# Expert tiles by pairs of 128-slot units with single units for odd rests, in a woven convolution and mixture-of-experts kernel

## The chip, the cores and the metric

The kernel runs on one core of one Trainium2 chip. TensorE (PE) multiplies matrices and transposes, VectorE (DVE) and ScalarE (ACT) work elementwise, GpSimd (POOL) issues indirect DMAs (gathers by a list of row numbers), SyncE (SP) issues plain ones. The metric is the device time of one execution in microseconds; lower is better. The time before is the median of three runs.

## What is computed

```python
x = x + conv(ln_c(x))            # three deformable 3x3 convolutions, each with relu; x is (4, 256, 64, 64)
t = to_tokens(x)                 # 4 images of 4096 tokens of 256 values
t = t + ffn(ln_t(t))
x = from_tokens(t)

def ffn(xf):                     # 8 experts, the best 2 of each token
    probs = softmax(xf @ gate_w + gate_b)
    top2_vals, top2_idx = top_k(probs, 2)
    cw = zeros((N, 8)); cw[token, top2_idx] += top2_vals
    out = 0
    for w1, b1, w2, b2, we in experts:      # 256 -> 512 -> 256
        out += we[:, None] * (gelu(xf @ w1 + b1) @ w2 + b2)
    return out
```

A deformable convolution samples the image at nine computed positions a pixel, bilinearly, before its matrix product. All data is float32.

## The kernel before

The convolutions run in twelve stages (`run`, one layer of one image each), each of eight blocks of 512 pixels with nine taps a block, 864 taps in all. A tap gathers four tiles of 128 pixels by indirect DMA on POOL (`g`, line 503, ten buffers), blends them on DVE (lines 509, 514) and ACT (517), transposes them on TensorE (`tp`, 532; copied out on ACT, 535) and multiplies them into `acc` (555).

The experts are woven into this. Tokens form five groups: images 0, 1, 2 whole (32 token blocks of 128, `M` = 32), image 3 in two halves (`M` = 16). When a group's last block has its tokens, `enqueue` puts its routing on a lane, then `begin` puts its expert tiles on the lane `tiles` and `end` its combination on the lane `sums`. At each tap `pump` gives each lane a credit of one tap; a piece runs once its cost is covered. A tile has three pieces of `pace`/3 taps, with paces 5, 5, 2, 1.5 and 0 for the five groups. After the last stage the lanes are emptied tile by tile (`drain`), which is the tail; there group 3 ends and group 4 runs.

`route` counts, on DVE with two matmuls, how many (token, choice) pairs each expert has, gives each pair a slot so that each expert starts on a multiple of `FT` = 256 slots, and derives for each tile of 256 slots its expert and the rows of its weights. A group has `NF = 2*M*128/256 + 7` tiles, 39 or 23, enough for every distribution over eight experts. `invert` makes from the slots, with one-hot matrices and matmuls into `inv`, the token of each slot.

A tile f is done by `expert` and the helpers:

- `fetch` (lines 800 and 812): one indirect DMA for the weights `w` of the tile's expert (two buffers, in turn by the step's parity), and `FU` = 2 for its 256 tokens, `zt`, 128 rows of 1 KB each. Row numbers beyond the table are skipped: where a tile has the same expert as the one before, its rows are set beyond it and nothing is moved. `order` alternates between the lower and upper half of the tiles, so that each half keeps one weight buffer.
- four transposes `ftp` (840), copied to `zT` on ACT (844);
- the first matrix product `ph` with 256 slots as moving columns (856), gelu to `hT` on ACT (866);
- the second, `py`, with the slots as stationary side and 256 output columns as moving side (874);
- `products` (892, 895): the bias added on DVE into `y`, stored by SP to the table `ys`.

Beside the convolution the next tile's fetch is issued before `py`; in the tail, before `ph`. POOL carries out its DMAs' issues in order, `g`, `w`, `zt` and the combination's gathers `gy` (915) in one queue. A scheduler orders each engine's instructions, so that parts of neighbouring tiles stand among each other. `combine` (930) gathers each token's two result rows from `ys` and adds them to the token with its weights; `give` transposes and stores.

The weights of one expert are 128 rows of 2308 values, 1.18 MB.

Of the kernel before, what the change touches and what calls it, by code (L numbers as in the profile page):

```python
# [82 lines left out]
class Group:  # L83


    def __init__(self, b, n0, n1):
        self.b, self.n0, self.n1 = b, n0, n1
        self.nm = f"{b}_{n0}"
        self.M = (n1 - n0) * TPB

        self.NF = 2 * self.M * P // FT + E - 1


        self.half = (self.NF + 1) // 2
        self.zt, self.acc, self.gy, self.sums, self.py = {}, [], [], [], None
        self.order = [s // 2 + s % 2 * self.half for s in range(self.NF)]


class Lane:
# [18 lines left out]
class Weave:  # L118
# [92 lines left out]
    def ffn_constants(self):  # L211
        nc, cst, ins = self.nc, self.cst, self.ins
        self.t_dram = [
            [
                self.dram.tile([P, TPB, C], F32, name=f"t_{b}_{n}", tag=f"t_{b}_{n}")
                for n in range(NB)
            ]
            for b in range(self.B)
        ]
        nf = max(g.NF for g in self.groups)  # L220
        for g in self.groups:
            g.zd = self.dram.tile([g.M * P, C], F32, name=f"z_{g.nm}", tag=f"z_{g.nm}")
        self.ys = [
            self.dram.tile([nf * FT, C], F32, name=f"ys_{i}", tag=f"ys_{i}") for i in range(3)
        ]
# [41 lines left out]
        assert FU * nf <= P  # L267
# [422 lines left out]
    def route(self, grp):  # L690

        nc, M, NF = self.nc, grp.M, grp.NF
        grp.slots = self.rt2.tile([P, 2, M], I32, tag="slots", bufs=3, name=f"slots_{grp.nm}")
        grp.tok = self.rt2.tile([P, FU * NF], I32, tag="tok", name=f"tok_{grp.nm}")
# [18 lines left out]
        )  # L713

        ni = small("ni", (P, E), I32)
        nc.vector.tensor_scalar(ni, slot[:, :, M - 1], float(FT - 1), None, ALU.add)
        nc.vector.tensor_scalar(ni, ni, FT_LOG, None, ALU.logical_shift_right)
        nt = small("nt", (P, E))
        nc.vector.tensor_copy(nt, ni)
        end = small("end", (P, E))  # L720
        nc.vector.tensor_tensor_scan(end, self.ones[:, :E], nt, 0.0, ALU.mult, ALU.add)
        off = small("off", (P, E))
        nc.vector.tensor_tensor(off, end, nt, ALU.subtract)
        nc.vector.tensor_scalar(off, off, float(FT), None, ALU.mult)
        nc.vector.tensor_tensor(slot, slot, tot, ALU.subtract)
        nc.vector.tensor_tensor(slot, slot, rp[:, 0], ALU.add)
        nc.vector.tensor_tensor(
            slot, slot, off.unsqueeze(2).to_broadcast([P, E, M]), ALU.add
        )
        for i in range(2):  # L730
            mine = small("r0", (P, E, M))
# [7 lines left out]
        past = small("r1", (P, NF, E))  # L739
        nc.vector.tensor_tensor(  # L740
            past,
            self.row_f[:, :NF].unsqueeze(2).to_broadcast([P, NF, E]),
            end.unsqueeze(1).to_broadcast([P, NF, E]),
            ALU.is_ge,
        )
        ex = small("ex", (P, NF))
        nc.vector.tensor_reduce(ex, past, AX.X, ALU.add)
        nc.vector.tensor_scalar(ex, ex, float(E - 1), None, ALU.min)

        rows = small("rows", (P, NF))  # L750
# [9 lines left out]
        for v, (op, k) in enumerate(((ALU.bitwise_and, P - 1), (ALU.logical_shift_right, 7))):  # L760
# [5 lines left out]
        grp.inv = self.ps1.tile([P, FU * NF], F32, tag="py", name=f"inv_{grp.nm}")  # L766

    def invert(self, grp, m):


        nc = self.nc
        lo, hi = grp.digits
        n = FU * grp.NF
# [16 lines left out]
    def fetch(self, grp, step):  # L790
# [15 lines left out]
            oob_is_err=False,  # L806
        )
        grp.zt[step] = []
        for u in range(FU):
            zt = self.ffn.tile([P, C], F32, tag=f"zt{u}", name=f"zt_{grp.nm}_{f}_{u}")  # L810
            j = FU * f + u
            self.nc.gpsimd.indirect_dma_start(  # L812
                out=zt,
                out_offset=None,
                in_=grp.zd,
                in_offset=bass.IndirectOffsetOnAxis(ap=grp.tok[:, j : j + 1], axis=0),
            )
            grp.zt[step].append(zt)
# [6 lines left out]
    def expert(self, grp, step):  # L825
# [8 lines left out]
        w = self.w[step % 2]  # L834
        w1, w2 = w[:, :W1N], w[:, W1N : W1N + W2N]
        zt = grp.zt.pop(step)
        tp = self.ps.tile([P, CC, FT], F32, tag="tp", name=f"ftp_{nm}")
        for u in range(FU):
            for c in range(CC):
                nc.tensor.transpose(  # L840
                    tp[:, c, u * P : (u + 1) * P], zt[u][:, c * P : (c + 1) * P], self.ident
                )
        zT = self.ffn.tile([P, CC, FT], F32, tag="zT", bufs=1, name=f"fzT_{nm}")
        nc.scalar.copy(zT, tp)  # L844
        yield

        beside = not self.draining
# [3 lines left out]
        for h0 in range(0, HC, 2):  # L851
            ph = self.ps1.tile([P, 2, FT], F32, tag="ph", name=f"ph_{nm}_{h0}")
            for h in range(2):
                for c in range(CC):
                    o = c * HID + (h0 + h) * P
                    nc.tensor.matmul(  # L856
                        ph[:, h, :],
                        lhsT=w1[:, o : o + P],
                        rhs=zT[:, c, :],
                        start=(c == 0),  # L860
                        stop=(c == CC - 1),
                    )
            ht = self.ffn.tile([P, 2, FT], F32, tag="hT", bufs=3, name=f"hT_{nm}_{h0}")
            for h in range(2):
                k = CC * HID + h0 + h
                nc.scalar.activation(ht[:, h, :], ph[:, h, :], AF.Gelu, bias=w1[:, k : k + 1])  # L866
            hT.append(ht)
        yield
        if beside:
            self.fetch_next(grp, step)  # L870
        py = self.ps1.tile([P, FU, C], F32, tag="py", name=f"py_{nm}")
        for u in range(FU):
            for h in range(HC):
                nc.tensor.matmul(  # L874
                    py[:, u, :],
# [7 lines left out]
    def products(self, grp):  # L883
# [3 lines left out]
        nc = self.nc  # L887
        f, py, w2 = grp.py
        grp.py = None
        y = self.ffn.tile([P, FU, C], F32, tag="y", name=f"y_{grp.nm}_{f}")  # L890
# [245 lines left out]
```

## Time and profile before

| | before |
|---|---|
| runs, us | 6805.82, 6795.70, 6805.55 |
| median, us | 6805.55 |
| profiled execution, us | 7520.62 |
| its span, us | 7518.9 |
| mean granted TensorE clock | 0.944 |
| instructions | 88985 |
| bytes moved | 2223.73 MB, mean 296 GB/s |
| gathers `g` on POOL | 3456, busy 3685.4 us |
| matmuls `acc` on PE | 6912, busy 3492.1 us |
| bias adds `y` on DVE | 163, mean 686 ns |

The profile is of one execution, which took 715 us longer than the median of the runs. The program counts each float32 matmul of the source as two on TensorE, and its transposes as one. Matmuls are pipelined, so that the sum of their busy time exceeds what they take back to back. "x" counts instructions; a group's line ends with its idle time before and what ended most of it. The experts run from about 2300 us of the span on; from about 7090 us on, the convolution's last gather is done and only experts are left.

### The profile page before, as it was taken

The numbers are of one execution on the slowest core, as the hardware profiler recorded it, in microseconds if no ns is written. First come the engines' busy times: TensorE is split into PE (matmuls) and PEld (weight loads), VectorE is DVE, ScalarE is ACT, GpSimd is POOL, SyncE is SP. The second block draws the span as 40 slices with busy tenths as digits, with TensorE's granted clock in tenths as the row PEclk, the third lists the DMA queues.
The fourth block names the chain that finished last, engine by engine and source line by source line (L and its number), as shares of the span: only waits on it lengthen the run. The fifth ranks groups of instructions, "written<-read, shape, count | busy, mean of one in ns | idle before, by whom it ended". The sixth has DMA issues, their size and how long they took to land.

```text
span 7518.9 us, 88985 instructions
## 1 busy us (share of the span) xinstructions
PE 6443.2 (86%) x26500; PEld 3618.8 (48%) x26500; DVE 4952.9 (66%) x11467; ACT 3266.0 (43%) x7141; POOL 4476.5 (60%) x4245
## 2 busy tenths in 40 slices
PE   6898888888898888889988888888888788977887
PEld 3443333334454444445554445444544555644565
DVE  6776777768887666567777556666768554667421
ACT  3444544445544444445443434444444333444322
POOL 4654666656666565556557656555656565666543
PEclk8999999999999999999999999999999899989998
DMA  8997999989998888888888888888888777888644
GB/s 266 337 325 274 352 342 335 346 331 356 362 349 311 300 305 297 278 315 322 314 293 316 293 280 314 295 302 294 308 306 299 251 271 240 288 302 287 211 139 123
DMA packets 800320, 2223.73 MB, mean 296 GB/s; under 512 B 104729, under 2 KB 302873, under 8 KB 794081
## 3 DMA queue, kind: packets, MB, share of 16 engines
q0 software_dynamic: 551200, 1947.35, 73.3%
q1 hardware_dynamic: 248640, 270.69, 10.9%
q8 instruction: 215, 3.52, 0.2%
q14 instruction: 265, 2.16, 0.1%
HBM read 2160.68 MB, written 196.40 MB: 313 GB/s over the span
## 4 chain that ended last, share of the span: by engine, by line
PE 69%; ACT 10%; issue 7%; another core or an unknown queue 6%; DVE 4%; DMA 2%; POOL 1%; SPq 0%; ACTq 0%; DVEq 0%; POOLq 0%
PE acc L555 34%; PE tp L532 10%; PE ph L856 7%; PE py L874 6%; PE po L357 6%; ACT sT L535 4%; ACT s L517 3%; DVE g L509 2%; DVE s L514 1%; PE pm L371 1%; ACT hT L866 1%; PE ftp L840 1%; ACT win L577 1%; PE tpv L325 1%
## 5 line engine op out<-in xcount | busy, mean ns | idle before, releaser
L503 POOL DMA_INDIRECT g<-tab,idx x3456 | 3685.4, 1066 | 2371.6 <-DVE s L514 1061.8
L555 PE MATMUL acc<-sT,wk 128*128 128x512 f32 x6912 | 3492.1, 620 | 253.4 <-ACT sT L535 147.5
L509 DVE SCALAR_TENSOR_TENSOR g<-g,cf 128x512 f32<-128x512 f32 x3456 | 2559.2, 742 | 269.1 <-DMA g<-tab,idx 245.5
L514 DVE SCALAR_TENSOR_TENSOR s<-g,cf 128x256 f32<-128x256 f32 x3456 | 1662.7, 483 | 1331.3 <-PE tp L532 729.9
L535 ACT COPY sT<-tp 128x512 f32<-128x512 f32 x1728 | 1002.0, 585 | 2312.0 <-PE tp L532 1553.0
L517 ACT ACTIVATE s<-s,cf 128x256 f32<-128x256 f32 x3456 | 1629.5, 508 | 256.7 <-DVE s L514 160.7
L555 PEld LDWEIGHTS acc<-sT,wk 128*128 128x128 f32 x6912 | 1198.9, 198 | 1106.7 <-issue 816.7
L532 PEld LDWEIGHTS tp<-ident,s 128*128 128x128 f32 x6912 | 893.2, 146 | 1666.2 <-issue 898.9
L532 PE MATMUL tp<-ident,s 128*128 128x128 f32 x6912 | 1287.3, 286 | 439.2 <-ACT s L517 253.8
L856 PE MATMUL ph<-fzT,w 128*128 128x256 f32 x2608 | 720.8, 411 | 78.0 <-ACT fzT L844 28.1
L874 PE MATMUL py<-w,hT 128*128 128x256 f32 x2608 | 671.1, 396 | 103.5 <-ACT hT L866 58.0
L856 PEld LDWEIGHTS ph<-fzT,w 128*128 128x128 f32 x2608 | 506.3, 205 | 212.9 <-issue 69.6
L874 PEld LDWEIGHTS py<-w,hT 128*128 128x128 f32 x2608 | 484.5, 196 | 242.0 <-issue 91.9
L866 ACT ACTIVATE hT<-ph,w 128x256 f32<-128x256 f32 x652 | 281.9, 471 | 616.3 <-PE ph L856 378.2
L812 POOL DMA_INDIRECT zt<-z,tok x326 | 333.8, 1024 | 161.5 <-issue 88.0
L800 POOL DMA_INDIRECT w<-in_W,wrow x163 | 178.0, 1092 | 381.2 <-issue 138.8
L357 PE MATMUL po<-win,wo 128*32 128x504 f32 (+1 forms) x2304 | 366.0, 615 | 6.5 <-ACT win L301 4.2
L892 DVE TENSOR_TENSOR y<-py,w 128x512 f32<-128x512 f32 x163 | 111.9, 686 | 341.5 <-PE py L874 285.1
L915 POOL DMA_INDIRECT gy<-ys,slots x256 | 255.6, 998 | 104.5 <-issue 70.0
L930 DVE SCALAR_TENSOR_TENSOR ta<-gy,cw,ta 128x256 f32<-128x256 f32 x256 | 120.6, 480 | 125.6 <-DMA gy<-ys,slots 78.4
L357 PE MATMUL po<-win_pre,wo 128*32 128x504 f32 (+1 forms) x1152 | 184.2, 617 | 2.0 <-ACT om L366 2.0
L366 ACT ACTIVATE om<-po,bo 128x512 f32<-128x512 f32 x96 | 65.9, 687 | 265.3 <-PE po L357 156.3
(154 smaller groups left out, 2961.0 us busy)
## 6 DMA issues: line engine op xcount, KB each, us to landing
tab<-hv SPq DMA_DIRECT2D x512, 128.0 KB
g<-tab,idx POOLq DMA_INDIRECT x3456
ys<-y SPq DMA_DIRECT2D x163, 256.0 KB
tab<-h_pre SPq DMA_DIRECT2D x128, 256.0 KB
wk<-in_conv_w SPq DMA_DIRECT2D x99, 256.0 KB
xc_pre<-in_x SPq DMA_DIRECT2D x32, 512.0 KB
xr_tok<-in_x SPq DMA_DIRECT2D x32, 512.0 KB
t<-t_tok SPq DMA_DIRECT2D x32, 512.0 KB
```

Source lines behind the costliest of these rows:

```text
L357: nc.tensor.matmul(po[g * Q : (g + 1) * Q, :].rearrange("q (r w) -> q r w", w=W)[:, :, x0:x1], lhsT=self.wo[l][:, 3 * ky + kx, c, :], rhs= ...
L503: self.gathered = nc.gpsimd.indirect_dma_start(out=g.rearrange("p x s f -> p (x s f)"), out_offset=None, in_=self.table(*self.stages[i]), ...
L509: nc.vector.scalar_tensor_tensor(g[:, :, 0, :], g[:, :, 1, :], cf[:, j, 0:1], g[:, :, 0, :], ALU.mult, ALU.add,)
L514: self.last = nc.vector.scalar_tensor_tensor(s, g[:, 1, 0, :], cf[:, j, 1:2], g[:, 0, 0, :], ALU.mult, ALU.add)
L517: nc.scalar.activation(s, s, AF.Copy, scale=cf[:, j, 2:3])
L532: self.turned = nc.tensor.transpose(tp[:, c, u * P : (u + 1) * P], ss[u][:, c * P : (c + 1) * P], self.ident)
L535: nc.scalar.copy(self.sT[:, :, t0 * P : (t0 + 2) * P], tp)
L555: nc.tensor.matmul(acc[:, o, :], lhsT=self.wk[k][:, c, o * P : (o + 1) * P], rhs=sT[:, c, :], start=(k == 0 and c == 0), stop=(k == K - 1 ...
L812: self.nc.gpsimd.indirect_dma_start(out=zt, out_offset=None, in_=grp.zd, in_offset=bass.IndirectOffsetOnAxis(ap=grp.tok[:, j : j + 1], axi ...
L856: nc.tensor.matmul(ph[:, h, :], lhsT=w1[:, o : o + P], rhs=zT[:, c, :], start=(c == 0), stop=(c == CC - 1),)
L866: nc.scalar.activation(ht[:, h, :], ph[:, h, :], AF.Gelu, bias=w1[:, k : k + 1])
L874: nc.tensor.matmul(py[:, u, :], lhsT=hT[h // 2][:, h % 2, u * P : (u + 1) * P], rhs=w2[:, h * C : (h + 1) * C], start=(h == 0), stop=(h == ...
```

## The change

Slots are now counted in units of 128. Each expert has its whole pairs of units (256 slots) and, where its units are odd in number, one single unit. The pairs of all experts come first, then, from `base` on, the single ones. A group has `NU = 2*M + 7` units, 71 or 39 (before, 78 or 46), as `NP` pairs (31 or 15) followed by nine singles: 40 or 24 tiles. Pairs beyond `NP` are worked as two singles. `units` gives a tile's first unit and how many it has, `route` gives each pair and each tile its place with a second count (`two`, `cut`, `off`, `end`, all doubled), and a single has one gather, half the columns in `ph`, half of `py` and half of `y`. A single's pieces cost half the pace. The weights are still skipped where the expert is that of the tile before in the order of f.

```diff
-        self.NF = 2 * self.M * P // FT + E - 1
+        self.NU = 2 * self.M + E - 1
+        self.NP = (self.NU - E - 1) // FU
+        self.NF = self.NP + E + 1
         self.half = (self.NF + 1) // 2
...
+    def units(self, f):
+
+        return (FU * f, FU) if f < self.NP else (f + self.NP, 1)
...
         ni = small("ni", (P, E), I32)
-        nc.vector.tensor_scalar(ni, slot[:, :, M - 1], float(FT - 1), None, ALU.add)
-        nc.vector.tensor_scalar(ni, ni, FT_LOG, None, ALU.logical_shift_right)
...
+        nc.vector.tensor_scalar(ni, slot[:, :, M - 1], float(P - 1), None, ALU.add)
+        two = small("two", (P, 2, E), I32)
+        nc.vector.tensor_scalar(two[:, 0], ni, FT_LOG, None, ALU.logical_shift_right)
+        nc.vector.tensor_scalar(
+            two[:, 1], ni, FT_LOG - 1, 1, ALU.logical_shift_right, ALU.bitwise_and
+        )
+        nt = small("nt", (P, 2, E))
+        nc.vector.tensor_copy(nt, two)
+        end = small("end", (P, 2, E))
+        for v in range(2):
+            nc.vector.tensor_tensor_scan(
+                end[:, v], self.ones[:, :E], nt[:, v], 0.0, ALU.mult, ALU.add
+            )
+        base = small("base", (P, 1))
+        nc.vector.tensor_scalar(
+            base, end[:, 0, E - 1 : E], float(FU), float(FU * grp.NP), ALU.mult, ALU.max
+        )
...
         nc.vector.tensor_tensor(slot, slot, rp[:, 0], ALU.add)
+        every = [P, E, M]
+        over = small("r1", (P, E, M))
+        nc.vector.tensor_tensor(over, slot, cut.unsqueeze(2).to_broadcast(every), ALU.is_ge)
         nc.vector.tensor_tensor(
-            slot, slot, off.unsqueeze(2).to_broadcast([P, E, M]), ALU.add
+            over, over, off[:, 1].unsqueeze(2).to_broadcast(every), ALU.mult
+        )
+        nc.vector.tensor_tensor(slot, slot, over, ALU.add)
+        nc.vector.tensor_tensor(
+            slot, slot, off[:, 0].unsqueeze(2).to_broadcast(every), ALU.add
         )
...
         ex = small("ex", (P, NF))
-        nc.vector.tensor_reduce(ex, past, AX.X, ALU.add)
+        part = small("exv", (P, NF))
+        for v in range(2):
+            past = small("r1", (P, NF, E))
...
+            nc.vector.tensor_reduce(part if v else ex, past, AX.X, ALU.add)
+        nc.vector.scalar_tensor_tensor(ex, ex, float(E), ex, ALU.is_lt, ALU.mult)
+        nc.vector.tensor_tensor(ex, ex, part, ALU.add)
...
         grp.zt[step] = []
-        for u in range(FU):
+        q, fu = grp.units(f)
+        for u in range(fu):
             zt = self.ffn.tile([P, C], F32, tag=f"zt{u}", name=f"zt_{grp.nm}_{f}_{u}")
-            j = FU * f + u
+            j = q + u
...
-        for u in range(FU):
+        for u in range(fu):
             for c in range(CC):
                 nc.tensor.transpose(
...
-        nc.scalar.copy(zT, tp)
+        nc.scalar.copy(zT[:, :, :n], tp[:, :, :n])
...
-                        ph[:, h, :],
+                        ph[:, h, :n],
                         lhsT=w1[:, o : o + P],
-                        rhs=zT[:, c, :],
+                        rhs=zT[:, c, :n],
...
-                nc.scalar.activation(ht[:, h, :], ph[:, h, :], AF.Gelu, bias=w1[:, k : k + 1])
+                nc.scalar.activation(
+                    ht[:, h, :n], ph[:, h, :n], AF.Gelu, bias=w1[:, k : k + 1]
+                )
...
-        for u in range(FU):
+        for u in range(fu):
             for h in range(HC):
                 nc.tensor.matmul(
                     py[:, u, :],
...
             nc.vector.tensor_tensor(
-                y, py, w2[:, HC * C :].unsqueeze(1).to_broadcast([P, FU, C]), ALU.add
+                y[:, :fu],
+                py[:, :fu],
...
-            self.ys[grp.i % 3][f * FT : (f + 1) * FT, :].rearrange("(u p) c -> p u c", u=FU),
-            y,
+            self.ys[grp.i % 3][q * P : (q + fu) * P, :].rearrange("(u p) c -> p u c", u=fu),
+            y[:, :fu],
...
             gen = self.expert(grp, step)
+            pace = grp.pace * grp.units(grp.order[step])[1] / FU
             for _ in range(3 + (step == 0)):
-                self.tiles.put(grp.pace / 3, lambda gen=gen: next(gen, None))
+                self.tiles.put(pace / 3, lambda gen=gen: next(gen, None))
```

More of the change, by code (lines that the diff above doesn't have):

```diff
@@ L219, in ffn_constants @@
         ]
-        nf = max(g.NF for g in self.groups)
+        nu = max(g.NU for g in self.groups)
         for g in self.groups:
@@ L223, in ffn_constants @@
         self.ys = [
-            self.dram.tile([nf * FT, C], F32, name=f"ys_{i}", tag=f"ys_{i}") for i in range(3)
+            self.dram.tile([nu * P, C], F32, name=f"ys_{i}", tag=f"ys_{i}") for i in range(3)
         ]
@@ L266, in ffn_constants @@
         nc.vector.tensor_copy(self.row_f, row_i)
-        assert FU * nf <= P
+        assert nu <= P
         self.token = cst.tile([P, NB * TPB], F32, name="token")
@@ L693, in route @@
         grp.slots = self.rt2.tile([P, 2, M], I32, tag="slots", bufs=3, name=f"slots_{grp.nm}")
-        grp.tok = self.rt2.tile([P, FU * NF], I32, tag="tok", name=f"tok_{grp.nm}")
+        grp.tok = self.rt2.tile([P, grp.NU], I32, tag="tok", name=f"tok_{grp.nm}")
         grp.wrow = self.rt2.tile([P, NF], I32, tag="wrow", name=f"wrow_{grp.nm}")
@@ L715, in route @@
         ni = small("ni", (P, E), I32)
-        nc.vector.tensor_scalar(ni, slot[:, :, M - 1], float(FT - 1), None, ALU.add)
-        nc.vector.tensor_scalar(ni, ni, FT_LOG, None, ALU.logical_shift_right)
[L718 to L722, printed above, removed]
-        nc.vector.tensor_tensor(off, end, nt, ALU.subtract)
@@ L724, in route @@
-        nc.vector.tensor_scalar(off, off, float(FT), None, ALU.mult)
+        nc.vector.tensor_scalar(ni, slot[:, :, M - 1], float(P - 1), None, ALU.add)
[7 more added lines that the diff above has]
+        end = small("end", (P, 2, E))
@@ new lines, in route @@
+        for v in range(2):
[6 more added lines that the diff above has]
+        )
+        off = small("off", (P, 2, E))
+        nc.vector.tensor_tensor(off, end, nt, ALU.subtract)
+        nc.vector.tensor_scalar(off[:, 0], off[:, 0], float(FT), None, ALU.mult)
@@ new lines, in route @@
+        nc.vector.tensor_scalar(off[:, 1], off[:, 1], base, float(P), ALU.add, ALU.mult)
+        cut = small("cut", (P, E))
+        nc.vector.tensor_scalar(cut, nt[:, 0], float(FT), None, ALU.mult)
+        nc.vector.tensor_tensor(off[:, 1], off[:, 1], cut, ALU.subtract)
+        nc.vector.tensor_tensor(off[:, 1], off[:, 1], off[:, 0], ALU.subtract)
+        nc.vector.tensor_scalar(end[:, 0], end[:, 0], float(FU), None, ALU.mult)
+        nc.vector.tensor_scalar(end[:, 1], end[:, 1], base, None, ALU.add)
@@ L737, in route @@
             nc.vector.tensor_copy(grp.slots[:, i, :], sf)
[L739 to L744, printed above, removed]
+        first = small("first", (P, NF))
+        nc.vector.tensor_scalar(first, self.row_f[:, :NF], float(grp.NP), None, ALU.add)
+        nc.vector.scalar_tensor_tensor(
+            first, self.row_f[:, :NF], float(FU), first, ALU.mult, ALU.min
         )
         ex = small("ex", (P, NF))
-        nc.vector.tensor_reduce(ex, past, AX.X, ALU.add)
+        part = small("exv", (P, NF))
+        for v in range(2):
+            past = small("r1", (P, NF, E))
+            nc.vector.tensor_tensor(
+                past,
+                first.unsqueeze(2).to_broadcast([P, NF, E]),
+                end[:, v].unsqueeze(1).to_broadcast([P, NF, E]),
+                ALU.is_ge,
+            )
+            nc.vector.tensor_reduce(part if v else ex, past, AX.X, ALU.add)
+        nc.vector.scalar_tensor_tensor(ex, ex, float(E), ex, ALU.is_lt, ALU.mult)
+        nc.vector.tensor_tensor(ex, ex, part, ALU.add)
         nc.vector.tensor_scalar(ex, ex, float(E - 1), None, ALU.min)
@@ L765, in route @@
             grp.digits.append(df)
-        grp.inv = self.ps1.tile([P, FU * NF], F32, tag="py", name=f"inv_{grp.nm}")
+        grp.inv = self.ps1.tile([P, grp.NU], F32, tag="py", name=f"inv_{grp.nm}")
     def invert(self, grp, m):
@@ L772, in invert @@
         lo, hi = grp.digits
-        n = FU * grp.NF
+        n = grp.NU
         for i in range(2):
@@ L836, in expert @@
         zt = grp.zt.pop(step)
+        fu = len(zt)
+        n = fu * P
         tp = self.ps.tile([P, CC, FT], F32, tag="tp", name=f"ftp_{nm}")
-        for u in range(FU):
+        for u in range(fu):
             for c in range(CC):
@@ L865, in expert @@
                 k = CC * HID + h0 + h
-                nc.scalar.activation(ht[:, h, :], ph[:, h, :], AF.Gelu, bias=w1[:, k : k + 1])
+                nc.scalar.activation(
+                    ht[:, h, :n], ph[:, h, :n], AF.Gelu, bias=w1[:, k : k + 1]
+                )
             hT.append(ht)
@@ L889, in products @@
         grp.py = None
+        q, fu = grp.units(f)
         y = self.ffn.tile([P, FU, C], F32, tag="y", name=f"y_{grp.nm}_{f}")
@@ L892, in products @@
             nc.vector.tensor_tensor(
-                y, py, w2[:, HC * C :].unsqueeze(1).to_broadcast([P, FU, C]), ALU.add
+                y[:, :fu],
+                py[:, :fu],
+                w2[:, HC * C :].unsqueeze(1).to_broadcast([P, fu, C]),
+                ALU.add,
             )
         nc.sync.dma_start(
-            self.ys[grp.i % 3][f * FT : (f + 1) * FT, :].rearrange("(u p) c -> p u c", u=FU),
-            y,
+            self.ys[grp.i % 3][q * P : (q + fu) * P, :].rearrange("(u p) c -> p u c", u=fu),
+            y[:, :fu],
         )
```

## The prediction

> **What bounds the kernel now.** I read the page first (busy shares, the chain that ended last, the costliest groups), then windows of the span, then the chain of waits in order of time near the end.
>
> ```profile
> PE 6443.2 (86%) x26500; PEld 3618.8 (48%) x26500; DVE 4952.9 (66%) x11467; ACT 3266.0 (43%) x7141; POOL 4476.5 (60%) x4245
> ...
> PE 69%; ACT 10%; issue 7%; another core or an unknown queue 6%; DVE 4%; DMA 2%; POOL 1%; SPq 0%; ACTq 0%; DVEq 0%; POOLq 0%
> PE acc L555 34%; PE tp L532 10%; PE ph L856 7%; PE py L874 6%; PE po L357 6%; ACT sT L535 4%; ACT s L517 3%; DVE g L509 2%; DVE s L514 1%; PE pm L371 1%; ACT hT L866 1%; PE ftp L840 1%; ACT win L577 1%; PE tpv L325 1%
> ...
> L856 PE MATMUL ph<-fzT,w 128*128 128x256 f32 x2608 | 720.8, 411 | 78.0 <-ACT fzT L844 28.1
> L874 PE MATMUL py<-w,hT 128*128 128x256 f32 x2608 | 671.1, 396 | 103.5 <-ACT hT L866 58.0
> L866 ACT ACTIVATE hT<-ph,w 128x256 f32<-128x256 f32 x652 | 281.9, 471 | 616.3 <-PE ph L856 378.2
> L812 POOL DMA_INDIRECT zt<-z,tok x326 | 333.8, 1024 | 161.5 <-issue 88.0
> L800 POOL DMA_INDIRECT w<-in_W,wrow x163 | 178.0, 1092 | 381.2 <-issue 138.8
> ```
>
> TensorE holds 69% of the chain, and the expert matmuls ph, py and ftp about 14% of the span, some 1050 us. Their busy means (411, 396 ns) overlap; the chain in order of time gives the back-to-back price (start, length, what):
>
> ```profile
> 7292.75 1.98 PE ph L856 x8
> 7295.28 0.70 PE py L874 x2
> 7295.98 1.73 PE ph L856 x8
> 7298.36 2.83 PE py L874 x12
> ```
>
> Eight ph in 1.73 us is 0.217 us each; the acc matmuls, of twice the columns, stand elsewhere in the same view at 0.43 us each, so time follows the moving columns. All TensorE groups at such prices (6912 acc at 0.43, 6912 tp at 0.11, 5216 expert matmuls at 0.217, 3456 po at 0.23, small ones 0.4 ms) come to about 6.08 ms. That is 81% of the profiled span, and 89% of the 6805 us median if the same stream runs there: TensorE is closer to the bound unprofiled than the profile shows.
>
> Stage by stage (columns: window, length, busy us and count for PE, PEld, DVE, ACT, POOL, granted clock, DMA share, GB/s):
>
> ```profile
> 1250.00:1500.00 250.00, 220.29 (x839) 99.66 (x837) 189.38 (x371) 122.03 (x270) 168.63 (x158) 0.99 0.94 347
> 2750.00:3000.00 250.00, 220.49 (x895) 123.77 (x894) 154.83 (x300) 112.38 (x250) 152.79 (x147) 0.96 0.87 297
> 7250.00:7500.00 250.00, 196.89 (x865) 156.72 (x866) 40.40 (x77) 55.87 (x127) 108.67 (x112) 0.90 0.44 135
> ```
>
> The first is convolution alone, and there DMA is full (0.94). In the second, expert tiles are woven in: DMA falls to 0.87, TensorE stays. Counting gather blends (L509) in these windows gives 158 against 126 per 250 us, so 1.58 against 1.98 us a gather, while 6.5 expert tiles (104 ph) run. A woven tile thus costs about (1.98-1.58)x126/6.5 = 7.8 us of time; the windows on both sides, with 122 and 121 gathers and 6.0 and 6.1 tiles, give 9.5 and 9.6, a mean of 8.9. The last window is the tail, experts alone, one tile each 8.2 us, with waits for weights:
>
> ```profile
> 7286.62 5.85 DMA w<-in_W,wrow
> ...
> 7312.91 9.14 DMA w<-in_W,wrow
> 7322.18 3.75 PE ph L856 x8
> ```
>
> After the 9.14 us wait the same eight ph take 3.75 us instead of 1.73.
>
> **What the Trainium skill says.** "TensorE: Matmul & The Clock Gate", Part 1: after an idle window of about 3.4 us the array runs at half rate until it has been busy as long; the 3.75 us after the wait agrees. Its section "Back-to-back issue gap": with a weight load per matmul, both set the spacing, so halving the columns need not halve the time. Here transposes of 128 columns stand at 0.11 us each with their own loads (tp, two in 0.22), which speaks for halving. "DMA: Bandwidth & Descriptors", "Anatomy of one DMA", gives 2.0 us plus bytes at 436 GB/s for a GpSimd DMA, an estimate of 4.7 us for 1.18 MB of weights; the waits in the trace put it at 6.1 to 9.3 us from issue to first use, and those count.
>
> **The change, part by part.** *Units.* Before: 3x78+2x46 = 326 units of 128 slots in 163 tiles. After: 3x71+2x39 = 291 units in 123 pairs and 45 singles, 168 tiles. A pair costs TensorE 4 transposes at 0.11, 16 ph and 16 py at 0.217: 7.4 us. A single has 2 transposes, 16 ph of 128 columns, 8 py of 256. If ph takes 0.11, that is 0.22+1.76+1.74 = 3.7 us, exactly half. Bounds on that ph: 0.11 from tp, and 0.205 from the LDWEIGHTS row if load and stream did not overlap, which adds 45x16x0.095 = 68 us. I take 0.11, since tp has the same load and columns. So 35 units x 3.7 = 130 us of stream go: 24 units beside the convolution (7 in each of the three large groups, 3 of group 3, whose first 12 tiles lie before the last tap in both programs' orders) and 11 in the tail.
>
> *Woven, 24 units.* 89 us, 93 at the clock of 0.95 to 0.96. What is late next are gathers and blends (DMA 0.87, DVE 0.62); the tile's price of 8.9 us against 7.4 of stream says nearly all passes. I take 0.8: -75. Bounds: 0.4 (-37), if gathers take over, and 24 x 4.45 = -107 at the full price of a woven tile.
>
> *Weights.* A load is skipped where the expert is the one before in the same half. The reference's fixed inputs give expert counts (group 0: 1048, 1094, 1024, 927, 1036, 939, 1074, 1050) from which the transfers follow: 9 a group before, 13, 12, 12, 13, 12 after, since each odd rest is another expert: 62 for 45. Of the 17, 11 fall in the weave. Each moves 1.18 MB, 3.9 us at 300 GB/s: +43 us of transfer, while 24 units fewer save 0.26 MB each of zt and ys, 21 us. Net 22 us on a queue at 0.87, with 12 us or more from fetch to use at those paces: I take +10, bounds 0 and +43.
>
> *Routing on DVE.* A large group gains about 13 small instructions at 0.18 us, three of 128x256 at 0.41, one compare and one reduction of 320 elements at 0.5 to 0.6: 4.6 us, a half group 3.5, 21 us in all. In the weave DVE's blends queue behind them, with ten gather buffers and four samples in hand as cover; I take +6, with 0 to +21 as bounds. ACT loses (163 tiles at 2.5 us become 123 plus 45 of about 1.7), POOL issues 30 DMAs fewer at 1.0 us; both have slack and count nothing.
>
> *Tail.* 11 units at 8.2/2 us: -45. The fetch of the next tile stands before the tile's ph and waits on DVE's y of the tile before; in the trace w is issued some 6.5 us ahead of the next ph. Behind a single that shrinks to about 3 us (3.7 of stream, 0.8 of gaps, 1.3 to issue). Seven loads follow a single there (steps 12, 16, 20 of group 3 and 8, 12, 16, 20 of group 4): 6.1 to 9.3 less 3, and some 1.5 of half-rate clock, 6 us each: +42. Other loads there stall less than the 22 us that three did before: -10. Longer routing +2. Tail: -11, bounds -45 and +30. While w waits in POOL's queue, zt and gy stand behind it, but zt runs two tiles ahead.
>
> Sum: -75+10+6-11 = -70. The profiled execution, 7520.6 us, would go to 7450. The runs' median is 715 us shorter, but the stream removed is the same work, so I carry the same 70 us: 6805.55-70 = 6735.
>
> **Rivals.** *Gathers take over.* If the unprofiled run is near the DMA limit (2224 MB in 6805 us is 327 GB/s, against 363 at most in a window), the weave returns only 0.4, -37, loads and routing cost +20, tail -3: -20, 6785. For: the balance of DMA and TensorE. Against: DMA share falls where tiles run.
>
> *Full price.* -107 in the weave, -45 in the tail, +10: -140, 6665. For: a woven tile costs more than its stream. Against: five tiles more, each with its waits.
>
> *Weight loads exposed (slower).* Each of the 17 extra loads stalls TensorE in its in-order queue, wherever a single comes soon after its fetch. It decides from (75+45-6)/17 = 6.7 us a load; at 8.5 us (wait plus half-rate clock) it is +145-114 = +31: 6835. For: the waits of 5.85 to 9.14 us. Against: 11 of them lie where tiles are 12 us or more apart.
>
> **How the numbers follow.** Forecast 6735, chance 0.60, own range 6695 to 6775; full price 0.08; gathers 0.18; exposed loads 0.14. The range 6668 to 6802 holds the forecast, the gather case and nearly all of full price. This kernel's measurement can tell about 0.2%, 14 us. Faster: 0.60+0.08+half of the gather case, 0.77; same 0.10; slower 0.13.
>
> **What would show it.** In the new profile: ph of 128x128 back to back at 0.11 us (at 0.2 the unit price was wrong); busy PE down by some 130 us less overlap; gathers per 250 us above 126 where group 0 runs; w waits in the tail after singles, at most 6 us each; more bytes in all by about 11 MB (17x1.18-35x0.26). PE idle before ph on w in the weave, many times, would make the slower case true; DMA share over 0.93 in the weave the gather case.

## The result, and the profile after

| | before | after |
|---|---|---|
| median of 6 runs each, us | 6804.50 | 6776.89 |
| lowest to highest, us | 6795.70 to 6812.24 | 6765.82 to 6790.49 |
| ratio, 95% interval | | 0.996, 0.9946 to 0.9973 |
| bytes moved, MB | 2223.73 | 2234.61 |

The change takes 28 us off (18 to 37 by the interval), where 70 were forecast: the right sign, less than half the size. 6777 lies inside the range given (6668 to 6802), near the rival "gathers take over" (6785).

In these runs and in twelve of the eighteen experiments the kernel before takes 6802 to 6806 us, but on the two chips of the other six it takes 7518 and 7648 us, and the profile that the prediction read is as long as that (7519 us). So the kernel before was profiled again, at 6801.5 us, and that profile is the one compared below.

"Weave" stands for the stretch in which expert tiles run beside the convolution, "stream" for what TensorE's matmuls take back to back. The page of the kernel before, profiled again (busy time, chain by engine, groups):

```profile
PE 6215.7 (91%) x26500; PEld 3522.8 (52%) x26500; DVE 4959.3 (73%) x11467; ACT 3276.6 (48%) x7141; POOL 4437.7 (65%) x4245
...
PE 73%; ACT 9%; DVE 7%; DMA 6%; issue 4%; POOL 2%; SPq 0%; ACTq 0%; DVEq 0%; POOLq 0%
...
L800 POOL DMA_INDIRECT w<-in_W,wrow x163 | 178.0, 1092 | 267.4 <-issue 110.4
```

The page of the kernel after (its chain was followed over the last 1% alone, so shares by engine can't be set beside these):

```profile
PE 6134.6 (91%) x26230; PEld 3430.6 (51%) x26230; DVE 4971.2 (73%) x11562; ACT 3261.7 (48%) x7160; POOL 4436.8 (65%) x4215
...
L897 PE MATMUL ph<-fzT,w 128*128 128x256 f32 (+1 forms) x2688 | 632.5, 370 | 60.6 <-DMA w<-in_W,wrow 29.1
L917 PE MATMUL py<-w,hT 128*128 128x256 f32 x2328 | 597.9, 392 | 40.7 <-ACT hT L907 30.9
L838 POOL DMA_INDIRECT w<-in_W,wrow x168 | 182.0, 1084 | 389.8 <-ACT hT L907 104.7
L851 POOL DMA_INDIRECT zt<-z,tok x291 | 298.9, 1027 | 131.8 <-issue 81.2
```

The instruction counts are those of the prediction: 168 x 16 = 2688 ph, 291 x 8 = 2328 py, 291 zt, and 10.9 MB more. PE is busy 81 us less. New are the waits in front of `w`: 267 us became 390.

Where the 28 us come from is read by stretches of taps. DVE's first blend (`g`, four a tap) runs 3456 times in each profile; a tap begins where the first of its four starts, and the tail begins with the last one. Us for each stretch, one profile a kernel:

| kernel | 0-324 | 324-432 | 432-540 | 540-612 | 612-738 | 738-756 | 756-864 | tail | span |
|---|---|---|---|---|---|---|---|---|---|
| before | 2207 | 780 | 802 | 523 | 908 | 169 | 988 | 424 | 6801.5 |
| after | 2211 | 778 | 802 | 509 | 930 | 147 | 991 | 409 | 6776.9 |
| new tiles in groups 0 to 2 alone | 2211 | 772 | 802 | 510 | 930 | 149 | 981 | 417 | 6771.9 |
| new tiles in groups 3 and 4 alone | 2214 | 776 | 805 | 521 | 911 | 163 | 1001 | 402 | 6792.1 |
| after, no loads for singles | 2215 | 780 | 802 | 514 | 929 | 146 | 990 | 406 | 6783.6 |
| after, pace 6 | 2210 | 755 | 784 | 527 | 889 | 128 | 1012 | 410 | 6714.8 |
| after, pace 5.9 | 2211 | 767 | 800 | 525 | 910 | 143 | 989 | 402 | 6747.5 |
| before, pace 5.45 | 2200 | 774 | 788 | 533 | 911 | 121 | 983 | 415 | 6725.2 |
| before, half of ph | 2207 | 775 | 786 | 521 | 886 | 168 | 991 | 420 | 6753.2 |
| before, half of zt | 2206 | 776 | 788 | 519 | 909 | 165 | 968 | 423 | 6753.7 |
| before, both halves | 2205 | 773 | 780 | 514 | 882 | 161 | 950 | 424 | 6688.7 |

Kernels with the same tiles and paces in a stretch differ there by 8 us at most (in the first stretch, of 2200 us, by 15), so a difference under 8 us says nothing. By their `y`, group 0's tiles lie on taps 326 to 516 before and 326 to 498 after, group 1's on 542 to 745 and 542 to 714, group 2's from 752 on. Where pairs alone run (324-432) nothing changes. Where group 1's singles lie, the new kernel is slower (612-738: +22), in three profiles alike; where group 0's lie it is no faster (432-540). It wins in 540-612 (-14), where group 0's combination now ends sooner (its gathers `gy` on taps 499 to 562 in place of 517 to 580), in 738-756 (-22), between groups 1 and 2, and in the tail (-15).

### The profile page after: what moved, and what is told of

It reads as the page before. It is cut to its first block, busy times and chain, and to the rows that moved or that the text cites. A ratio compares the mean times of both kernels' runs of the same rounds, so it can differ in the third digit from the quotient of the medians.

```text
span 6776.9 us, 88526 instructions
## 1 busy us (share of the span) xinstructions
PE 6134.6 (91%) x26230; PEld 3430.6 (51%) x26230; DVE 4971.2 (73%) x11562; ACT 3261.7 (48%) x7160; POOL 4436.8 (65%) x4215
## 2 busy tenths in 40 slices
DMA packets 794958, 2234.61 MB, mean 330 GB/s; under 512 B 102792, under 2 KB 296456, under 8 KB 786544
## 5 line engine op out<-in xcount | busy, mean ns | idle before, releaser
L559 PE MATMUL acc<-sT,wk 128*128 128x512 f32 x6912 | 3404.9, 605 | 170.5 <-ACT sT L539 159.6
L559 PEld LDWEIGHTS acc<-sT,wk 128*128 128x128 f32 x6912 | 1159.7, 192 | 966.0 <-issue 635.4
L897 PE MATMUL ph<-fzT,w 128*128 128x256 f32 (+1 forms) x2688 | 632.5, 370 | 60.6 <-DMA w<-in_W,wrow 29.1
L917 PE MATMUL py<-w,hT 128*128 128x256 f32 x2328 | 597.9, 392 | 40.7 <-ACT hT L907 30.9
L897 PEld LDWEIGHTS ph<-fzT,w 128*128 128x128 f32 x2688 | 461.9, 198 | 183.3 <-ACT fzT L885 53.8
L917 PEld LDWEIGHTS py<-w,hT 128*128 128x128 f32 x2328 | 422.4, 193 | 160.8 <-ACT hT L907 78.7
L907 ACT ACTIVATE hT<-ph,w 128x256 f32<-128x256 f32 (+1 forms) x672 | 271.4, 441 | 468.3 <-PE ph L897 454.9
L851 POOL DMA_INDIRECT zt<-z,tok x291 | 298.9, 1027 | 131.8 <-issue 81.2
L936 DVE TENSOR_TENSOR y<-py,w 128x512 f32<-128x512 f32 (+1 forms) x168 | 103.0, 613 | 269.0 <-PE py L917 269.0
L885 ACT COPY fzT<-ftp 128x512 f32<-128x512 f32 (+1 forms) x168 | 88.7, 528 | 183.2 <-PE ftp L881 181.0
```

The costliest lines, as they stand in the source:

```text
L559: nc.tensor.matmul(acc[:, o, :], lhsT=self.wk[k][:, c, o * P : (o + 1) * P], rhs=sT[:, c, :], start=(k == 0 and c == 0), stop=(k == K - 1 ...
L851: self.nc.gpsimd.indirect_dma_start(out=zt, out_offset=None, in_=grp.zd, in_offset=bass.IndirectOffsetOnAxis(ap=grp.tok[:, j : j + 1], axi ...
L897: nc.tensor.matmul(ph[:, h, :n], lhsT=w1[:, o : o + P], rhs=zT[:, c, :n], start=(c == 0), stop=(c == CC - 1),)
L907: nc.scalar.activation(ht[:, h, :n], ph[:, h, :n], AF.Gelu, bias=w1[:, k : k + 1])
L917: nc.tensor.matmul(py[:, u, :], lhsT=hT[h // 2][:, h % 2, u * P : (u + 1) * P], rhs=w2[:, h * C : (h + 1) * C], start=(h == 0), stop=(h == ...
```

## The experiments

**Weave or tail.** TAIL and WEAVE say where the missing gain was lost. The kernel before ran once more beside them (6803.21 us).

> The kernel before, unchanged, for a second profile: the first one (span 7518.9 us) was 715 us longer than the median of the runs. Both theories expect a profiled span near 6800 us with a granted clock near 0.975, and so a profile that can be laid beside the one after. If the gain is eaten in the tail (theory TAIL), the convolution's last gather comes about 60 us later here than after, and the tail from there to the end is shorter here than after by some 30 us. If the weave returns little (theory WEAVE), the last gather comes only some 20 us later and the tails are alike within 10 us.

> New tiles in groups 0 to 2 alone, the old 256-slot tiles in groups 3 and 4 (the longer routing instructions stay in all five). TAIL: the weave's part stands alone, about -60 us, 6745. WEAVE: about -20 us, 6785.

> New tiles in groups 3 and 4 alone, old tiles in groups 0 to 2. TAIL: the waits for weights behind single tiles cost more than eleven units save, +30 us, 6835. WEAVE: about -10 us, 6795.

```diff
-        self.groups = [Group(b, 0, NB) for b in range(last)]
-        self.groups += [Group(last, 0, NB // 2), Group(last, NB // 2, NB)]
+        self.groups = [Group(b, 0, NB, True) for b in range(last)]
+        self.groups += [Group(last, 0, NB // 2, False), Group(last, NB // 2, NB, False)]
```

The flag says whether a group has the new tiles; tail only has it the other way round. Weave only: 6786.67 us, ratio 0.9976 (0.9967 to 0.9985), 16 us less. Tail only: 6800.09, 0.9999 (0.9991 to 1.0008), 2 us less. Both carry the longer routing of all five groups, which alone costs 10 us (below). Without it the new tiles save some 26 us in the weave, where 65 were forecast (-75+10), and some 12 in the tail, where 13 were: estimates from three medians, good to about 8 us. So the weave holds the miss. In the two profiles neither TAIL nor WEAVE has its signs in full: the last gather comes 9 us later before than after (6371 and 6362 us), and the tail behind it is 15 us longer before.

**The singles' loads.**

> The kernel after, with the weights of every single tile left out: a single is multiplied with what its buffer holds, so part of the output is not the reference's. Instructions are the same but for one small memset a group; some 4 transfers of 1.18 MB a group are gone. TAIL: the odd steps' loads go but those of pairs behind singles stay, so half of the tail's loss comes back: 6755. If extra loads cost much in the weave as well: 6730. WEAVE (gathers and blends set the pace, loads are hidden): within 10 us of after, 6770.

```diff
+        nc.vector.memset(same[:, grp.NP :], 1.0)
```

6785.33 us, 0.9971 (0.9959 to 0.9983), as the change with its loads (0.9946 to 0.9973), with 24.8 MB less moved, 21 loads, and the stretches with singles stay as long (432-540: 802, 612-738: 929). The seventeen added loads cost nothing that can be measured; the rival "weight loads exposed" is out.

**What a woven tile's parts cost.** GATHERS and SLACK are two views of what takes over beside the convolution once TensorE's stream shrinks.

> The kernel before with the second half of each ph sum left out in groups 0 to 2 (eight of sixteen ph matmuls a tile, so the output is not the reference's): 117 tiles x 8 x 0.217 = 203 us of TensorE stream less, thinned evenly over the same taps, with no transfer, no tile and no routing changed. GATHERS (transfers set the pace of the weave throughout, TensorE is not the bound): under 60 us gained, above 6745. SLACK (TensorE is the bound at taps that hold a tile, and only taps without one are bound by gathers, so that stream counts when it is thinned out but not when taps are emptied): most of it, 6620 to 6650.

> The kernel before with the weights moved for every tile of groups 0 to 2, none skipped (one DVE instruction a group left out): 90 transfers of 1.18 MB more, about 106 MB, 300 us of transfer at 350 GB/s. GATHERS: +150 us or more, above 6950. SLACK: the transfers fit beside TensorE's tiles, +30 to +80, 6830 to 6880.

> The longer routing code of the change in all five groups, but every tile still of 256 slots with the old counts: 21 us more of DVE work and nothing else. Both theories: 0 to +10 us, 6802 to 6812; a larger loss would mean that the routing, not the tiles, ate the gain.

```diff
-                for c in range(CC):
+                parts = 1 if grp.i < 3 else CC
+                for c in range(parts):
...
-        nc.vector.scalar_tensor_tensor(rows, same, float(E * P), rows, ALU.mult, ALU.add)
+        if grp.i > 2:
+            nc.vector.scalar_tensor_tensor(rows, same, float(E * P), rows, ALU.mult, ALU.add)
```

The diffs are the first two; the third keeps the old tiles and has the new `route` for all groups. Half of ph: 6760.5 us, 0.9941 (0.9926 to 0.9956): 203 us less stream (117 tiles x 8 x 0.217) returned 45 us, a share of 0.22, where GATHERS put it. All loads: 6819.21, 1.0021 (1.0013 to 1.003): 106 MB more cost 14 us, far less than either theory had. Routing: 6815.52, 1.0017 (1.001 to 1.0025): +10 us, where 6 + 2 were forecast.

So bytes are not what takes over. The next pair asks whether GpSimd's queue is:

> The kernel before in which the tiles of groups 0 to 2 gather only the first 128 of their 256 tokens and use them twice: 117 gathers zt fewer on GpSimd's queue (1.03 us of issue each, 120 us) and 31 MB less moved; TensorE's stream stays. QUEUE (what takes over when the stream shrinks is GpSimd's queue of issues, which the gathers of the samples share with zt and w): 40 to 100 us below before, more than the 45 us that 203 us of TensorE's stream gave. CHAIN (neither stream nor queue, but the waits between the pieces of a tile and the taps, which go with how often a tile stands in a tap): 0 to 15 us below before.

> Both halvings of the kernel before in groups 0 to 2: the second half of the sums of ph left out (203 us of TensorE's stream) and the second gather of zt (120 us of GpSimd's issues). QUEUE with TensorE as the next bound: more than the two alone added, 100 to 200 us below before. CHAIN: the two alone added, 45 to 60 us below.

```diff
-        for u in range(FU):
+        for u in range(1 if grp.i < 3 else FU):
             zt = self.ffn.tile([P, C], F32, tag=f"zt{u}", name=f"zt_{grp.nm}_{f}_{u}")
...
-                    tp[:, c, u * P : (u + 1) * P], zt[u][:, c * P : (c + 1) * P], self.ident
+                    tp[:, c, u * P : (u + 1) * P], zt[u % len(zt)][:, c * P : (c + 1) * P], self.ident
```

Half of zt: 6752.81 us, 0.9924 (0.991 to 0.9937), 53 us for 120 us of issue, a share of 0.44; the page has 15.4 MB less moved, not 31. Both: 6694.53, 0.9843 (0.9829 to 0.9856), 111 us against 45 + 53. Both fall where QUEUE put them, the second at its low end; the 13 us beyond the plain sum lie within what the three intervals leave open. The place tells more: in taps 756 to 864 half of ph alone brings nothing (991 for 988), half of zt 20 us, both 38. In 612-738 half of ph brings 22 us, half of zt nothing, both 26; in 432-540 it is 16, 15 and 22, less than the sum. So some stretches hang on TensorE's stream, others on the path of the gathers, and in group 2's the first shows only when the second is eased. That is the reading that fits, from one profile each; the bytes, though part of the same path, are not its tight part.

**Thinner tiles.** The new groups 0 and 1 leave taps free at their ends (group 0 is done 18 taps sooner), so that their tiles can be spread.

> The kernel after with the pace of groups 0 and 1 at 6 taps a pair in place of 5, so that the fewer units are spread over 213 taps (before: 195; after: 177) and no taps are left without a tile between groups. SLACK: the 14 units of these groups then pay nearly their stream, and what singles crowd is thinned: 30 us below after, 6745. GATHERS: same as after within 8 us, 6777.

> As d_before545 (the kernel before, paces 5.45 in place of 5 in the first two groups), on a chip whose time for the kernel before is near 6805 us. KNEE: 6765 to 6790. ALIGN: 6795 to 6810.

> As d_pace59 (the changed kernel with paces 5.9 in place of 5 in the first two groups), on a chip whose time for the kernel before is near 6805 us. KNEE: 6700 to 6728, within 15 us of pace 6. ALIGN: 6765 to 6785.

```diff
-        for i, (g, pace) in enumerate(zip(self.groups, (5.0, 5.0, 2.0, 1.5, 0.0))):
+        for i, (g, pace) in enumerate(zip(self.groups, (6.0, 6.0, 2.0, 1.5, 0.0))):
```

Pace 6: 6713.26 us, 0.9868 (0.9853 to 0.9883), 92 us below before and 64 below the change, where SLACK had 30. Pace 5.9: 6750.37, 0.9921 (0.9907 to 0.9934), less than halfway, which neither theory gave. The old kernel at 5.45: 6739.44, 0.9909 (0.9893 to 0.9924), 66 us below before and better than KNEE's lowest value, but not where its tiles were thinned: taps 324 to 738 take 3006 us for 3014, and 48 us are gained in the eighteen taps 738 to 756. Both theories fall as they stood. In taps 324 to 738 the changed kernel gains 18 us from pace 5.9 and 65 from pace 6 (3020, 3002, 2955). That pace 6, whose pieces fall on whole taps, stands alone there speaks for ALIGN in this stretch; no other pace with whole taps was run, so it is not shown. What happens between groups 1 and 2 can be seen. The waits of the kernel before, in taps 732 to 750 (5183 to 5330 us):

```profile
ACT o L954 <- PE otp L948: 29.3, 1, 29.3
...
DVE ta L930 <- DMA gy<-ys,slots: 13.4, 7, 6.5
...
POOL zt L812 <- DVE tok L788: 9.9, 1, 9.9
```

There group 1's combination (`gy`, `ta`, `o`) meets group 2's routing. The first `zt` of group 2 waits 9.9 us for its token numbers at the head of the queue that the gathers `g` use; group 1's last `py` starts just behind these numbers, at 5266 us, and `y`, its store and the gathers `gy` follow one after the other. Taps 744 to 748 alone took 56 us; after the change 25, and with pace 5.45 33. Of the thirteen profiles of 6689 to 6818 us, the seven with the old tiles and paces in groups 0 and 1 have 52 to 56 us there, the other six 25 to 35. So where a group's combination falls is worth some 20 to 30 us, and both versions move it. That it makes the whole of the 22 and 48 us in taps 738 to 756 was not shown.

**Runs on chips of the longer kind.** The first four of these runs fell on a chip where the kernel before takes 7517.72 us, the last two on one where it takes 7647.74.

> The kernel before with its own 39 tiles of 256 slots a group, paces of the first two groups 5.45 in place of 5, so that the tiles of a group lie on about 212 taps in place of 193: as few tiles per tap as fit before the next group begins, and pieces that don't fall on whole taps. KNEE (what a tile costs rises steeply with tiles per tap, whatever the tiles' form, so thinning pays by itself; fewer units only leave room for it): about 6775, 20 to 40 us below before. ALIGN (the 64 us of pace 6 came from pieces that fall on whole taps): 6795 to 6810, as before.

> The changed kernel with paces of 5.9 in place of 5 in the first two groups: nearly as thin as pace 6, but pieces every 1.97 taps, which don't fall on whole taps. KNEE: within 15 us of the 6713 of pace 6, so 6700 to 6728. ALIGN: 6765 to 6785, as the change at pace 5.

> The changed kernel with paces 6, 6 and 2.5 in place of 5, 5 and 2: the third group, the densest, lies on taps 758 to 835 in place of 757 to 819. KNEE: 15 to 30 us below the 6713 of pace 6, if the third group's combination and the fourth group's tiles are not pushed into the tail; 6685 to 6700. If they are, the tail grows by what the weave saves: 6705 to 6725. ALIGN (2.5 falls on no whole taps, as 2 doesn't): 6705 to 6720.

> The changed kernel with the singles of the first two groups paced like pairs, which spreads each group's 40 tiles on 197 taps in place of 175, the same taps as the 39 of the kernel before: the removed units thin the tiles' second half, where singles lie, in place of leaving taps without tiles at the end. KNEE: 6745 to 6760, since a third of pace 6's thinning is had, where the taps were slowest. If only whole taps count (ALIGN), or only pairs' thinning: 6770 to 6785.

> The changed kernel in which the 27 singles of groups 0 to 2 do the work of a pair (two gathers of the same tokens, 256 columns in every product, the bias on both units; only the first unit is stored), at the changed kernel's places and paces. It measures what halving a tile saves. UNIT (the prediction's price: 3.7 us of stream a single, 0.8 of it time): 27 x 3.0 = 80 us above the changed kernel, about 6857. PARTS (what the two halvings measured: 0.38 us for a half of the stream of ph, as much for py, 0.45 us for a zt): 27 x 1.2 = 33 us above, about 6810. TILE (a woven tile costs by its pieces and waits, hardly by its columns): 0 to 15 us above, 6777 to 6792.

> As d_pace6_25 (the changed kernel with paces 6, 6 and 2.5 for the first three groups), on a chip whose time for the kernel before is near 6805 us. If the dense tiles of the third group cost as those of the first two do when thinned: 6685 to 6705. If their combination is only pushed into the tail: 6705 to 6730.

```diff
-            pace = grp.pace * grp.units(grp.order[step])[1] / FU
+            one = grp.i > 1 and grp.units(grp.order[step])[1] == 1
+            pace = grp.pace / FU if one else grp.pace
```
```diff
-        for u in range(fu):
+        for u in range(FU if grp.i < 3 else fu):
             zt = self.ffn.tile([P, C], F32, tag=f"zt{u}", name=f"zt_{grp.nm}_{f}_{u}")
-            j = q + u
+            j = q + min(u, fu - 1)
```

The first diff is d_flat's, the second g_full_singles'. Ratios to before on the same chip: 1.0208 (1.0179 to 1.0237) at pace 5.45, 1.0128 (1.01 to 1.0157) at 5.9, 1.0095 (1.0063 to 1.0126) and, on the other chip, 1.0135 (1.0099 to 1.017) at 6, 6, 2.5, 1.0144 (1.0113 to 1.0175) with flat singles, 1.0217 (1.0184 to 1.025) with full singles. All are slower than before there, among them two that elsewhere are 0.8 and 0.9% faster. The change itself was not run on such a chip. So none of these tells KNEE from ALIGN, and what halving a single saves stays unmeasured.

They show something else. The waits of the whole execution, changed kernel at pace 5.9 on such a chip (us in total, times, longest):

```profile
ACT sT L539 <- remote: 376.1, 86, 15.1
DVE s L518 <- remote: 275.3, 93, 12.1
ACT hT L907 <- remote: 157.9, 32, 9.2
```

and the first profile, the one that the prediction read:

```profile
ACT sT L535 <- remote: 371.9, 89, 12.0
DVE s L514 <- remote: 220.2, 93, 12.0
ACT hT L866 <- remote: 123.6, 30, 10.1
```

"Remote" is a release by nothing that this core's profile holds, and the kernel has one core. Counted on ScalarE over the execution, waits of this kind above 2 us come to 134 with 686 us in the first profile, 138 with 750 us at pace 5.9, and none in the kernel before profiled again or in its pace 5.9 counterpart above: most of the 717 and 877 us by which the profiles of each kernel differ, if a pause costs its length. In a chain of waits they are pauses of about 6 us (pace 5.9, in group 2's stretch):

```profile
6129.87 5.99 another core or an unknown queue
6168.77 6.10 another core or an unknown queue
```

## Why the size was wrong

**TensorE as the bound, 6.08 ms of stream.** Half right: it is busy for 91% of the span in both kernels, but 203 us taken evenly out of its stream gave back 45. Its busy time fell by 81 us where some 130 us of stream were taken out; it counts overlap, as foreseen.

**Half price of a single, ph of 128 columns at 0.11 us.** Right, in the tail's chain of the kernel after (start, length, what):

```profile
6586.28 7.82 DMA w<-in_W,wrow
6594.15 3.80 PE ph L897 x8
...
6606.61 0.89 PE ph L897 x8
...
6621.63 8.43 DMA w<-in_W,wrow
...
6657.76 6.31 DMA w<-in_W,wrow
6664.11 2.88 PE ph L897 x8
...
6690.11 5.79 DMA w<-in_W,wrow
```

Eight of a single's ph in 0.89 us are 0.11 each.

**"The tile's price of 8.9 us against 7.4 of stream says nearly all passes. I take 0.8: -75."** This is the step that failed, in two ways.

The price was wrong. It came from the profile with 686 us of pauses. In the profile of 6801.5 us, taps 342 to 522 take 131.9 us per 18 with 3.5 tiles (35 `y` in ten such stretches), taps 126 to 324 without tiles 114.6: a tile costs (131.9-114.6)/3.5 = 5.0 us, well below its own stream of 7.4. The pauses fell unevenly: of those above 2 us on ScalarE, the prediction's window without tiles (1250 to 1500 us) holds one of 4.6 us, its three windows with tiles (2500 to 3250 us) hold fifteen with 68 us. If a pause costs its length, that alone puts some (68/3-4.6)/6.2 = 2.9 us on each tile, an estimate. So a good part of the stream lies in time that the gathers need anyway, and the halving of ph says how much of stream alone comes back: 0.22. Even 0.4, the lower bound given, was too high for stream alone. In the weave as a whole, -16 less the routing's 10 leaves some 26 us for 21 units, 1.2 us each where the forecast had 3.1.

The place was wrong too. The sum took the units out of the taps where tiles run. But a single's pieces cost half the pace, so two singles take the taps of one pair, and the number of units per tap stays. Taps 648 to 714 of the kernel before, where group 1's last tiles lie, then of the kernel after, where its singles lie (window, then busy us and count of PE, PEld, DVE, ACT, POOL, clock, DMA share, GB/s; below, groups of that window):

```profile
4579.00:5050.00 471.00, 435.69 (x1785) 256.21 (x1784) 370.96 (x823) 250.88 (x530) 314.43 (x306) 0.99 0.94 344
...
L509 DVE SCALAR_TENSOR_TENSOR g<-g,cf 128x512 f32<-128x512 f32 x265 | 196.5, 742 | 3.4 <-DMA g<-tab,idx 3.4
...
L874 PE MATMUL py<-w,hT 128*128 128x256 f32 x210 | 54.7, 388 | 6.1 <-ACT hT L866 6.1
...
L800 POOL DMA_INDIRECT w<-in_W,wrow x14 | 14.9, 1062 | 4.7 <-DMA g<-tab,idx 1.4 <-issue 1.2 <-ACT s L517 0.9
```

```profile
4565.00:5055.00 490.00, 441.65 (x1845) 259.06 (x1844) 374.08 (x826) 254.51 (x552) 317.97 (x309) 0.99 0.90 339
...
L513 DVE SCALAR_TENSOR_TENSOR g<-g,cf 128x512 f32<-128x512 f32 x264 | 195.5, 743 | 18.8 <-DMA g<-tab,idx 18.3
...
L917 PE MATMUL py<-w,hT 128*128 128x256 f32 x216 | 57.5, 392 | 2.1 <-ACT hT L907 2.1
...
L838 POOL DMA_INDIRECT w<-in_W,wrow x17 | 18.9, 1111 | 50.6 <-DVE g L513 17.5 <-ACT s L521 10.1 <-DVE pr_tok L672 9.0
```

210 py are 26 units, 216 are 27: no stream was saved here, and there are 17 fetches in place of 14. PE is busy for 92.5% of the time before and 90.1% after. POOL now stands idle 51 us in front of the fetches of `w`, before 5; the gathers stand behind them in its queue, and DVE waits 18 us for gathered pixels, before 3. That is the size of the 19 us by which the stretch grows. At paces 5.9 and 6 POOL's wait there falls to 20 and 11 us, DVE's to nothing, and the stretch to 469 and 452 us; but these paces thin the tiles as well, and no run took the wait away alone. Among group 0's singles (taps 432 to 498) it is as long (57 us, before 4) where the stretch grows by 5 only. Of the taps left without tiles, 498 to 540 gave 6 us and 714 to 738 none. What the change won in the weave it won behind them, in 540-612 and 738-756, where no unit had been taken out.

**Weights, +10.** Measured at nothing: without the singles' loads the time is the same, and 106 MB cost 14 us, so that the 13 MB of eleven loads would cost 2.

**Routing, +6 in the weave, +2 in the tail.** +10 us measured for both, 7 to 17 by the interval. Right.

**Tail, -11.** Right as a sum, within the noise: -2 with the routing of all groups, so some -12 without it against -13. In the chain above, `w` lands late, 5.8 to 8.4 us, and the next eight ph take 2.9 to 3.8 us instead of 1.73, as foreseen. But PE's waits for `w` behind the last gather grew by 8 us only, before and after (us in total, times, longest):

```profile
PE ph L856 <- DMA w<-in_W,wrow: 21.3, 7, 7.6
```

```profile
PE ph L897 <- DMA w<-in_W,wrow: 29.1, 10, 5.5
```

What the two large terms, -45 for the units and +42 for the waits, came to one by one was not measured; that their sum held may be luck.

**The rival "gathers take over".** Nearest in time, and in part in kind: its weave was -37, and the path of the gathers does stand close to TensorE. But it had the limit in the bytes, and more bytes hardly cost; its sign, a DMA share over 0.93, was no sign, for the kernel before has 0.94 in the taps shown. **Carrying 70 us from 7520 to 6806 us** was the error behind the price: the pauses were 9% of that profile, and the page named them ("another core or an unknown queue 6%").

## What to carry to other kernels

Before a price is drawn from a profile, its span is set against the runs, and waits released by nothing that the kernel has are added up; here a tile of 5.0 us looked like 8.9. Work taken out of a stage whose pacing goes by units does not thin the stage, it ends it sooner, and pays only what that changes in the taps that follow: the same change gave 28 us with the old pace and 92 with one that spreads the tiles over the freed taps, on chips like those of the result. Most of that is the pace's: the old tiles with a pace of their own gave 66. Halving a resource's work, each alone and both, stretch by stretch, says more than its busy time: the share that returns was 0.22 for the stream and 0.44 for the issues.

## What was not expected of the hardware

- On two chips the same kernel takes 7518 and 7648 us in place of 6802 to 6806, with 134 to 167 pauses of about 5 us on ScalarE in the profiles of that length. There, versions of this kernel that win 0.8 to 0.9% elsewhere lose 1.3 to 2.1%. "Runtime: NRT & Kernel Launch" of the Trainium skill, section "Instruction fetch mechanics", says that engines fetch their instructions by DMA in blocks, mostly hidden. The trace speaks against it here: of the 134 pauses of the first profile 33 overlap one of its some 480 transfers marked `instruction`, and shifted in time they would overlap 42 on average. The pauses stay open.
- 106 MB of weights in rows of 9.2 KB, added where the DMA share was 0.91 (taps 324 to 864), cost 14 us, 0.13 us a MB; at the 327 GB/s of the kernel before they would take 324 us alone.
- A busy TensorE need not be the bound: in taps 774 to 820 of the kernel before it is busy for 442 of 458 us, and half of ph, 208 matmuls or 45 us of its stream, took 7 us off (windows before and with half of ph, columns as above):

```profile
5568.00:6026.00 458.00, 442.01 (x1971) 296.95 (x1970) 273.93 (x564) 214.01 (x461) 292.28 (x289) 1.00 0.84 292
```

```profile
5526.00:5977.00 451.00, 411.92 (x1747) 258.55 (x1748) 273.83 (x562) 218.01 (x458) 288.25 (x289) 0.97 0.85 295
```
